# Attention and quantised feed-forward on one core: the exponentials' scores as one 72-row product a head, four heads' maxima in one run

## The chip, the cores and the metric

The kernel runs on one core of a Trainium2 chip. The time is device microseconds of one execution, and the number told is the median of several runs. TensorE multiplies into PSUM (8 banks of 128 partitions x 512 f32), ScalarE and VectorE read PSUM, GpSimd works on SBUF alone, and transfers are issued from the queues of SyncE (SP) and GpSimd (POOL).

## The reference

One pre-norm transformer layer on x of 2 x 1024 x 512 in f32, with 32 heads of 16 columns, and a feed-forward part of 1376 columns with ternary weights and rounded activations:

```python
x = x + attn(layernorm(x), w_q, w_k, w_v, w_o)
x = x + ffn(layernorm(x), w_gate, w_up, w_down, s_gate, s_up, s_down)

# attn
q, k, v = (proj(w_q), proj(w_k), proj(w_v))          # b, 32 heads, 1024, 16
scores = einsum('bhqd,bhkd->bhqk', q, k) / sqrt(16.)
attn = softmax(scores, axis=-1)
out = einsum('bhqk,bhkd->bhqd', attn, v)             # then w_o
# ffn
xq = int4_quant(x)
gate = square(relu(bitlinear(xq, w_gate, s_gate)))
inter = int8_quant(bitlinear(xq, w_up, s_up) * gate)
return bitlinear(inter, w_down, s_down)
```

## The kernel before

The attention is cut into 32 **steps**: two batches, two halves of 512 queries, four groups of 128 columns (8 heads), and in each group two sets of four heads (s = 0 and 1). A step is cut into 8 **slots** (`NT`). The main loop counts slots with T. In slot T it does three things for three places in the row of steps:

- **Maxima** of step T // 8. For each head the scores of 128 queries by 512 keys are made (`max_mm`, L590), and VectorE reduces two heads at once, 128 x 1024, to the negated row maxima (`max_reduce`, L600). After eight slots `max_parts` joins the pieces into `mcols`, and `max_rows` (L613, L617) turns them into rows with four products against the identity and a ScalarE copy `mrow`.
- **Exponentials** of the step that had slot T - 10 (`LE`). The scores are made again the other way round, 128 keys by 512 queries, the maximum is subtracted in the same accumulation, and ScalarE takes the exponential of two heads at once (`exp_mm` L630, `exponentials` L634). `j` = 0 is heads 0 and 1, `j` = 1 heads 2 and 3.
- **Values** (`weigh_values`, L660) for the exponentials of slot T - 1: for each of four heads the 128 keys by 32 columns of `vt` are multiplied with the exponentials, accumulated over the eight slots in one PSUM bank (`pso`); columns of ones beside the values give the denominators.

Numbers are split into a high and a low part (`hi`, `lo`) in the format f32r, which TensorE takes in one pass; plain f32 takes more. For each head `kst` holds 32 rows: 16 of the high part of k and 16 of the low part. `qst[n][0]` and `qst[n][1]` hold the high and the low part of q, each twice. So a score is two products of 32 rows, and four heads lie in four 32-row tiles of the array. The subtraction of the maximum is a third product of two rows, `onesr` by `mrow`. The parts come from DRAM (`kD`, `qD`), where the projections put them, by `load_k` (L567) and `load_q` (L573).

The order on every engine is the order in which the program emits instructions (a manual schedule). A slot before is:

1. `scores(exps[:1], maxs[:1])`: exponentials j = 0 mixed with maxima of heads 2 and 3 in three passes.
2. `weigh_values` of the slot before.
3. `scores(exps[1:], maxs[1:])`: exponentials j = 1 mixed with maxima of heads 0 and 1.
4. In the first slot of a new step `max_parts`, in the second `max_rows`.
5. **Fillers** (`fill.run`): pieces of all other work, the projections (L476, L533), layer norms, output projection (L847) and feed-forward (L937, L1006), handed out by a budget of 960 to 1800 ns a slot and by due times in slots. Their products go to a PSUM bank of their own, and ScalarE, VectorE or GpSimd take them from there.

Score tiles come from a ring of three, each of two banks (`scores_psum`). Loads for a step are emitted some five slots ahead (`load_slot`), on SP's queue, where the stores of projections, the small transfers of `normalise` and the transposes of the feed-forward part stand as well. At the end `the_end` finishes the last 512 tokens in an order of its own, in buffers that it takes over from the loop (`place`).

Of the kernel before, what the change touches and what calls it, by code (L numbers as in the profile page):

```python
# [10 lines left out]
F32 = mybir.dt.float32  # L11
# [5 lines left out]
ALU = mybir.AluOpType  # L17
# [216 lines left out]
def kernel(  # L234
# [65 lines left out]
    nc.vector.tensor_copy(onesr, eye)  # L300
    ones = onesr.bitcast(F32)

    lowrow = const.tile([P, 1], F32, name="lowrow")
    nc.vector.memset(lowrow, -1.0)
    for i in range(4):
        nc.vector.memset(lowrow[32 * i : 32 * i + 16, :], 0.0)
    second = const.tile([P, 1], I32, name="second")
    nc.vector.memset(second, 1)
    for i in range(4):
# [1 line left out]
    negmagic = const.tile([P, 1], F32, name="negmagic")  # L311
    nc.vector.memset(negmagic, -MAGIC)

    mcols = [const.tile([P, TQ, P], F32R, name=f"mcols{k}") for k in range(2)]
    vst = [const.tile([P, 2, 4, 4, 32], F32, name=f"vst{k}") for k in range(1)]
    for m in mcols:
        nc.gpsimd.memset(m.bitcast(F32), 0.0)
    for v in vst:
        for s in range(2):
            nc.gpsimd.memset(v[:, s, :, :, 16 * (1 - s) : 16 * (1 - s) + 16], 1.0)  # L320
# [15 lines left out]
    def scores_psum(name):  # L336
        return ps_s.tile([P, 2, QB], F32, tag="s", name=name)
# [29 lines left out]
    def norm_inputs(b, half, fast, need=()):  # L367
# [45 lines left out]


    qD = {
        (b, g, h): dram.tile([2, 8 * 32, QB], F32, name=f"qD_{b}_{g}_{h}")
        for b in range(B)
        for g in range(NG)
        for h in range(NQ)
    }  # L420
    kD = {(b, g): dram.tile([8 * 32, S], F32, name=f"kD_{b}_{g}") for b in range(B) for g in range(NG)}
    vD = {
        (b, g, s): dram.tile([P, NT, P], F32, name=f"vD_{b}_{g}_{s}")
        for b in range(B)
# [35 lines left out]
    def project_qk(b, g, which, h, have, fast=False, first=False):  # L460
# [34 lines left out]
        if first:  # L495

            for s in range(2 - which):
                for l, part in enumerate((hi, lo)):
                    for a in range(2 - which):
                        for r in range(4):  # L500
                            src = part[32 * r + 16 * s : 32 * r + 16 * s + 16, :].bitcast(F32)
                            at = 32 * r + 16 * (l if which else a)
                            dst = kst[0][:, h * QB : (h + 1) * QB] if which else qst[s][l]
                            queue = (nc.sync, nc.gpsimd)[l if which else a]
                            queue.dma_start(dst[at : at + 16, :].bitcast(F32), src)  # L505
                yield ("copied",)
            if which == 0:
                return
        queue = nc.gpsimd if fast and not first else nc.sync
        for l, part in enumerate((hi, lo)):  # L510
            if which == 0:
                dst = qD[b, g, h][l].rearrange("(e a d) q -> a e d q", a=2, d=16)
                for a in range(2):
                    queue.dma_start(dst[a], part.bitcast(F32))
            else:
                dst = kD[b, g].rearrange("(e l d) q -> l e d q", l=2, d=16)[l]
                queue.dma_start(dst[:, :, h * QB : (h + 1) * QB], part.bitcast(F32))
            yield ("gap", 1)

    def step_k(n):  # L520
        b, _, g, s = steps[n]
        return kD[b, g].rearrange("(r s e) q -> s r e q", r=4, s=2)[s]

    def project_v(b, g, half, have):
        w, wait = proj_weights("v", b, g, f"wv_{b}_{g}_{half}")
# [34 lines left out]
    pm, mrow, probs = {}, {}, {}  # L560

    def places(n):
        kst[n] = sb.tile([P, S], F32R, tag="kst", name=f"kst_{n}", bufs=3)
        qst[n] = [sb.tile([P, QB], F32R, tag="qst", name=f"qst_{n}_{l}", bufs=6) for l in range(2)]

    def load_k(n, first=0):
        nc.sync.dma_start(kst[n][:, first:].bitcast(F32), step_k(n)[:, :, first:])  # L567
# [1 line left out]
    def load_q(n):  # L569
        b, h, g, s = steps[n]  # L570
        for l, q in enumerate(qst[n]):
            rows = qD[b, g, h][l].rearrange("(r s e) q -> s r e q", r=4, s=2)[s]
            nc.sync.dma_start(q.bitcast(F32), rows)  # L573

    def load_v(n):
        b, h, g, s = steps[n]
# [25 lines left out]
    def max_parts(n):  # L602
        m = sp.tile([P, TQ, 4], F32, tag="m", name=f"m_{n}")
        p = pm.pop(n)
        nc.vector.tensor_tensor(m, p[:, :, 0, :], p[:, :, 1, :], ALU.min)
        cols = mcols[n % 2].rearrange("p t (r c) -> p t r c", r=4)
        nc.vector.tensor_copy(cols[:, :, :, 0], m)
        nc.vector.tensor_tensor(cols[:, :, :, 1], m, cols[:, :, :, 0].bitcast(F32), ALU.subtract)

    def max_rows(n):  # L610
        ps = scores_psum(f"psn_{n}")[:, 0, :]
        for t in range(TQ):
            nc.tensor.matmul(  # L613
                ps[:, t * P : (t + 1) * P], mcols[n % 2][:, t, :], identr, start=True, stop=True
            )
        mrow[n] = sb.tile([P, QB], F32R, tag="mrow", name=f"mrow_{n}", bufs=2)
        nc.scalar.copy(mrow[n], ps)  # L617

    probs = {}

    def exp_mm(n, i, j, ps, l):
        for r in (2 * j, 2 * j + 1):
            rows = slice(32 * r, 32 * r + 32)
            if l < 2:
                left, right = kst[n][rows, i * P : (i + 1) * P], qst[n][l][rows, :]
            else:

                rows = slice(32 * r, 32 * r + 2)
                left, right = onesr[rows, :], mrow[n][rows, :]
            nc.tensor.matmul(ps[:, r % 2, :], left, right, start=(l == 0), stop=(l == 2))  # L630

    def exponentials(n, i, j, ps):
        e = sb.tile([P, 2, QB], F32, tag="e", name=f"e_{n}_{i}_{j}", bufs=4)
        nc.scalar.activation(e, ps, AF.Exp, scale=SCALE)  # L634
        probs.setdefault((n, i), {})[j] = e

    def scores(exps, maxs):


        es = [(*x, scores_psum(f"pse_{x[0]}_{x[1]}_{x[2]}")) for x in exps]  # L640
        ms = [(*x, max_tile(*x)) for x in maxs]
        for l in range(3):
            for x in es:
                exp_mm(*x, l)
            if l or not es:
                for x in ms:
                    max_mm(*x, l - bool(es)) if l - bool(es) < 2 else None
        for x in es:
            exponentials(*x)
        for x in ms:  # L650
            max_reduce(*x)

    acc, po, OT = {}, {}, {}

# [95 lines left out]
    def load_raw(m, i, name):  # L750
        ap, parts = mats[m]
        c, n, rows, cols = parts[i]
        t = sb.tile([P, 512], F32, tag="raw", name=f"{name}{m}_{c}_{n}", bufs=4)
        nc.gpsimd.dma_start(t[:rows, :cols], ap[c * P : c * P + rows, n : n + cols])
        return t

    def weight_sums():
# [2 lines left out]
            nc.gpsimd.memset(wsum[m], 0.0)  # L760
        todo = [(m, i) for m in range(3) for i in range(len(mats[m][1]))]
        raw = deque()
        for k in range(len(todo) + 4):
            if k >= 4:
                m, i = todo[k - 4]
                c, n, rows, cols = mats[m][1][i]
                junk = sb.tile([P, 512], BF16, tag="junk", name=f"junk{m}_{i}", bufs=1)
                nc.scalar.activation(
                    junk[:rows, :cols],
                    raw.popleft()[:rows, :cols],  # L770
                    AF.Abs,
                    accum_out=wsum[m][:rows, i : i + 1],
                )
            if k < len(todo):
                raw.append(load_raw(*todo[k], "raw"))
            yield ("gap", 1)
# [266 lines left out]
    def the_end(n):  # L1043
# [74 lines left out]
        def place(tag, shape, k, bufs):  # L1118
            return [sb.tile(shape, F32, tag=tag, name=f"end_{tag}_{j}", bufs=bufs) for j in range(k)]

        quad = [t.bitcast(BF16) for t in place("qst", [P, QB], TQ, 6)]
        xqs, xT = [q[:, :H] for q in quad], [q[:, H:].rearrange("p (c t) -> p c t", c=KC) for q in quad]
        xns = place("raw", [P, 512], TQ, 4)
        v = place("inter", [P, I], 2, 2)
        for half in range(2):
            v.append(place(f"xnT{half}", [P, KC * QB], 1, 1)[0][:, :I])
        iq = [sb.tile([P, FC * P], BF16, tag="iq", name=f"end_iq_{j}", bufs=2) for j in range(2)]
        iq += [t.bitcast(BF16)[:, :I] for t in place("v", [P, NT * P], 2, 2)]
        pairs = place("e", [P, 2, QB], 4, 4)
        iqT = [t.bitcast(BF16)[:, : FC * P] for t in place("kst", [P, S], 3, 3)]  # L1130
        iqT.append(pairs.pop().rearrange("p j q -> p (j q)").bitcast(BF16)[:, : FC * P])
        g2 = [t[:, j, :] for t in pairs for j in range(2)]

        def inputs(i):
# [151 lines left out]
    ps = scores_psum("warm")  # L1286
    for k in range(WARM):
        nc.tensor.matmul(
            ps[:, k % 2, :], onesr, mcols[0].rearrange("p t c -> p (t c)"), start=True, stop=True
        )  # L1290
    fill.kind = "s"
    now(firsts[0])
# [107 lines left out]
    for T in range(LE + NT * NSTEP + 1):  # L1400
# [4 lines left out]

        fill.scores = int(T < LE - 1 or T >= NT * NSTEP)

        n = T // NT + 1
        if 1 < n < NSTEP and T == load_slot(n):
            b, h, g, s = steps[n]  # L1410
# [8 lines left out]
            load_v(n)  # L1419
        if im == 0 and 0 < nm <= NSTEP:  # L1420
            max_parts(nm - 1)
        exps = [(ne, ie, j) for j in range(2)] if 0 <= ne < NSTEP else []
        maxs = [(nm, im, j) for j in (1, 0)] if nm < NSTEP else []
        mixed = bool(exps and maxs)
        if mixed:
            scores(exps[:1], maxs[:1])
        elif exps:
            scores(exps, [])
        if 0 <= nw < NSTEP:
            weigh_values(nw, iw)  # L1430
            if iw == NT - 1 and nw % 2 and nw < NSTEP - 1:
# [3 lines left out]
                fill.add("tokens", first_tokens(nw), (), "ffn", 0)  # L1435
        feed()
        fill.run(100.0, short=True)
        if mixed:
            scores(exps[1:], maxs[1:])
        elif maxs:  # L1440
            scores([], maxs)
        if im == 1 and 0 < nm <= NSTEP:
            max_rows(nm - 1)
        share = min(max(fill.pace([w[4:] for w in ffns]), SHARE), MORE)
        left = fill.run(share + min(left, SHARE))

    while ffns or fill.left():
        feed()
# [49 lines left out]
```

## Time and profile before

| | before |
|---|---|
| median of 3 runs | 1179.4 us (1176.8 to 1182.54) |
| span of the profiled execution | 1179.7 us |
| TensorE busy | 1154.8 us, 98% |
| VectorE busy | 868.8 us, 74% |
| ScalarE busy | 686.8 us, 58% |
| GpSimd busy | 264.1 us, 22% |
| bytes moved by DMA | 135.35 MB |
| mean granted TensorE clock | 0.999 |

The profiled execution has no time of its own beside its span; the span lies within the three times. Busy time of TensorE is modelled at its ends, and products in different tiles of the array overlap, so the sum of its groups' durations is more than its busy time; starts of instructions are a better measure. In the rows of groups, the numbers behind the bar are busy time and mean duration in ns, and behind the second bar the idle time of the engine just before, with what ended it. `PEld` is TensorE's loading of weights.

### The profile page before, as it was taken

The page shows a single profiled execution, that of the slowest core. Times are in us where ns is not written, and L with a number is a line of the kernel's source. Part 1 is how long each engine was busy: PE and PEld are TensorE (multiplying, and loading weights), DVE is VectorE, ACT ScalarE, POOL GpSimd, SP SyncE. Part 2 cuts the span into 40 slices and gives each one's busy share as a digit, 9 for nine tenths or more (in the row PEclk, how much of TensorE's full clock was granted, in tenths as well). Part 3 has the DMA queues.
Part 4 walks back from the last instruction along what each step waited for, and adds up shares of the span by engine and source line. Part 5 has one row for each costly group of instructions (what it writes and reads, how often), then busy time and mean ns, then how long its engine had stood idle before and what let it go on. Part 6 is the DMA issues. An engine that isn't in the chain of part 4 may idle for free.

```text
span 1179.7 us, 21990 instructions
## 1 busy us (share of the span) xinstructions
PE 1154.8 (98%) x8922; PEld 522.5 (44%) x8922; DVE 868.8 (74%) x1261; ACT 686.8 (58%) x878; POOL 264.1 (22%) x319
## 2 busy tenths in 40 slices
PE   8899999999999999999999999999999999999998
PEld 5454444544444444544444445444444433444344
DVE  6765577898876677788866665786988788888467
ACT  2058765556565556566665555465666555665746
POOL 3224336465501101221011011022110001220111
PEclk9999999999999999999999999999999999999999
DMA  5666765556623323443633324244442516362300
GB/s 157 174 183 194 249 197 176 172 190 197 194 93 96 103 55 110 113 95 77 94 86 121 124 59 147 84 130 138 84 97 60 89 53 83 58 81 55 79 9 37
DMA packets 97099, 135.35 MB, mean 115 GB/s; under 512 B 34829, under 2 KB 54285, under 8 KB 96997
## 3 DMA queue, kind: packets, MB, share of 16 engines
q1 hardware_dynamic: 87204, 105.75, 34.6%
q0 software_dynamic: 9792, 28.19, 7.7%
q8 instruction: 70, 1.15, 0.4%
q14 instruction: 33, 0.26, 0.1%
HBM read 89.25 MB, written 37.19 MB: 107 GB/s over the span
## 4 chain that ended last, share of the span: by engine, by line
PE 81%; DVE 5%; DMA 5%; issue 2%; POOL 2%; SPq 2%; ACT 2%; POOLq 0%; DVEq 0%; ACTq 0%
PE pse L630 25%; PE pso L660 18%; PE psm L590 9%; PE psv L533 4%; PE psk L476 4%; PE psy L847 4%; PE psq L476 4%; PE pu L937 2%; PE py L1006 2%; DVE pm L600 2%; PE pg L937 2%; DMA rden<-rD 1%; PE psn L613 1%; SPq L505 1%; PE end L1161 1%
## 5 line engine op out<-in xcount | busy, mean ns | idle before, releaser
L600 DVE TENSOR_REDUCE pm<-psm 128x2 f32<-128x1024 f32 x512 | 623.8, 1222 | 242.9 <-PE pse L630 146.0
L634 ACT ACTIVATE e<-pse 128x1024 f32<-128x1024 f32 x512 | 522.7, 1023 | 408.2 <-PE pse L630 307.3
L590 PE MATMUL psm<-kst,qst 32*128 32x512 f32 x2048 | 369.5, 444 | 7.3 <-DMA kst<-kD 3.8
L630 PE MATMUL pse<-qst,kst 32*128 32x512 f32 x2048 | 367.6, 442 | 3.9 <-DVE pm L600 3.1
L630 PEld LDWEIGHTS pse<-qst,kst 32*128 32x128 f32 x2048 | 149.2, 183 | 332.8 <-issue 199.7
L660 PE MATMUL pso<-e,v 128*32 128x512 f32 x2048 | 272.9, 605 | 0.0
L630 PE MATMUL pse<-mrow,onesr 2*128 2x512 f32 x1024 | 203.9, 396 | 0.0
L590 PEld LDWEIGHTS psm<-kst,qst 32*128 32x128 f32 x2048 | 151.3, 183 | 25.5 <-ACT e L634 10.8
L630 PEld LDWEIGHTS pse<-mrow,onesr 2*128 2x128 f32 x1024 | 94.5, 183 | 3.3
L951 POOL TENSOR_TENSOR g<-g 128x460 f32<-128x460 f32 (+1 forms) x36 | 34.7, 964 | 244.7 <-ACT g L947 237.4
L660 PEld LDWEIGHTS pso<-e,v 128*32 128x32 f32 x2048 | 40.4, 108 | 94.4 <-issue 93.7
L807 POOL TENSOR_SCALAR low<-raws,whalf 128x512 bf16<-128x512 f32 (+2 forms) x35 | 52.0, 1488 | 30.5 <-DMA raws<-in_wuT 8.1
L476 PE MATMUL psq<-xnT,wq 128*128 128x512 f32 x112 | 57.8, 626 | 0.0
L533 PE MATMUL psv<-wv,xnT 128*128 128x128 f32 x384 | 53.2, 285 | 0.0
L533 PEld LDWEIGHTS psv<-wv,xnT 128*128 128x128 f32 x384 | 45.9, 191 | 12.5 <-issue 11.7
L847 PE MATMUL psy<-wo,OT 128*128 128x512 f32 x96 | 49.6, 625 | 0.0
L476 PE MATMUL psk<-xnT,wk 128*128 128x512 f32 x96 | 49.5, 624 | 0.0
L699 POOL TENSOR_TENSOR OT<-po,rden 128x512 f32<-128x512 f32 x15 | 19.2, 1278 | 99.5 <-PE pse L630 52.8
L547 POOL DMA_DIRECT2D vD<-vst x30 | 16.7, 559 | 110.5 <-ACT vst L545 107.8
L909 POOL TENSOR_SCALAR xn<-x,mv,a 128x512 f32<-128x512 f32 x12 | 25.1, 2089 | 71.5 <-DVE a L885 71.5
L937 PEld LDWEIGHTS <-xqT 128*128 128x128 bf16 x288 | 22.4, 98 | 37.8 <-issue 23.8
L937 PE MATMUL pg<-wg,xqT 128*128 128x460 fp8e4 (+1 forms) x144 | 34.2, 360 | 0.0
(227 smaller groups left out, 945.1 us busy)
## 6 DMA issues: line engine op xcount, KB each, us to landing
v<-vD SPq DMA_DIRECT2D x32, 512.0 KB
kst<-kD SPq DMA_DIRECT2D x31, 512.0 KB
qst<-qD SPq DMA_DIRECT2D x60, 256.0 KB
vD<-vst POOLq DMA_DIRECT2D x30, 256.0 KB, 5.7
qD<-hi_q SPq DMA_DIRECT2D x28, 256.0 KB
qD<-lo_q SPq DMA_DIRECT2D x28, 256.0 KB
x<-in_x SPq DMA_DIRECT2D x20, 256.0 KB
rden<-rD SPq DMA_DIRECT2D x15, 256.0 KB
```

What stands on the lines that cost most here:

```text
L476: nc.tensor.matmul(ps, w[:, c, :], xnT[b, h][:, c, :], start=(c == 0), stop=(c == KC - 1))
L533: nc.tensor.matmul(ps[:, i * P : (i + 1) * P], xnT[b, half][:, c, i * P : (i + 1) * P], w[:, c, :], start=(c == 0), stop=(c == KC - 1),)
L590: nc.tensor.matmul(ps[:, r % 2, :], qst[n][l][rows, t * P : (t + 1) * P], kst[n][rows, kh * QB : (kh + 1) * QB], start=(l == 0), stop=(l = ...
L600: nc.vector.tensor_reduce(pm[n][:, t, kh, 2 * j : 2 * j + 2], ps, AX.X, ALU.max, negate=True)
L630: nc.tensor.matmul(ps[:, r % 2, :], left, right, start=(l == 0), stop=(l == 2))
L634: nc.scalar.activation(e, ps, AF.Exp, scale=SCALE)
L660: nc.tensor.matmul(acc[n][32 * r : 32 * r + 32, :], vt[n][:, i, r, :], e[r // 2][:, r % 2, :], start=(i == 0), stop=(i == NT - 1),)
L807: nc.gpsimd.tensor_scalar(low, w, h[:rows, m, 1:2], None, ALU.is_lt)
L847: nc.tensor.matmul(ps, OT[b, h, g][:, i * P : (i + 1) * P], wo[g], start=(g == 0), stop=(g == NG - 1),)
L909: nc.gpsimd.tensor_scalar(xn, xt, mean, a, ALU.subtract, ALU.mult)
L937: nc.tensor.matmul(ps, xT[:, c, :], w[:, c, n : n + size], start=(c == 0), stop=(c == KC - 1))
L951: nc.gpsimd.tensor_tensor(g2[j], g2[j], g2[j], ALU.mult)
```

## The change

The exponentials' scores of a head become one product of 72 rows. For this k is stored twice in `kD` (`a` = 0, 1) and q with its parts in one tile, so that 64 rows hold high and low of k, twice, against high of q twice and low of q twice: all four parts of the score in one contraction. Eight more rows subtract the maxima: rows 64 to 71 of `qm` hold the maxima rows of all four heads (copied by ScalarE, four times side by side), and the same rows of `kw` hold ones for the head's own pair and zeros for the others (`subtraction_rows`, once). `kw` holds two slots' keys for four heads and is loaded every second slot, two slots ahead; `qm` is loaded once a step.

The maxima stay products of 32 rows, but all four heads are made in one run. The order in a slot is now maxima, values of the slot before, exponentials j = 0, `max_rows` (in a step's first slot), fillers, exponentials j = 1. `kst` has 2 buffers where it had 3, `qst` 4 where it had 6, `e` 2 where it had 4, `raw` 3 where it had 4, `mcols` 1 where it had 2; the first query's parts are stored to `qD` as well; and `the_end` takes other buffers.

```diff
-    mcols = [const.tile([P, TQ, P], F32R, name=f"mcols{k}") for k in range(2)]
+    MROW = 64
+    mcols = const.tile([P, TQ, P], F32R, name="mcols")
...
             else:
-                dst = kD[b, g].rearrange("(e l d) q -> l e d q", l=2, d=16)[l]
-                queue.dma_start(dst[:, :, h * QB : (h + 1) * QB], part.bitcast(F32))
+                dst = kD[b, g].rearrange("(e a l d) q -> l a e d q", a=2, l=2, d=16)[l]
+                for a in range(2):
+                    queue.dma_start(dst[a][:, :, h * QB : (h + 1) * QB], part.bitcast(F32))
...
+    kw = [const.tile([P, 4, 2 * P], F32R, name=f"kw{k}") for k in range(2)]
...
+    def subtraction_rows():
+
+        pick = sp.tile([P, 4], F32, tag="rstd1", name="pick")
+        pairs = ident[:, MROW : MROW + 8].rearrange("p (r c) -> p r c", c=2)
+        nc.vector.tensor_reduce(pick, pairs, AX.X, ALU.add)
+        src = pick[MROW : MROW + 8, :].rearrange("p (r o) -> p r o", o=1)
+        for k in kw:
+            nc.vector.tensor_copy(k[MROW : MROW + 8, :, :], src.to_broadcast([8, 4, 2 * P]))
+
+    def load_kw(n, p):
+
+        b, h, g, s = steps[n]
+        src = kD[b, g].rearrange("(r s e) q -> s e r q", r=4, s=2)[s][:, :, 2 * P * p : 2 * P * (p + 1)]
+        nc.sync.dma_start(kw[p % 2][:64].bitcast(F32), src)
+
+    def load_qm(n):
+
+        b, h, g, s = steps[n]
+        qm[n] = sb.tile([P, 4, QB], F32R, tag="qm", name=f"qm_{n}", bufs=2)
+        src = qD[b, g, h].rearrange("(r s e) q -> s e r q", r=4, s=2)[s]
+        nc.sync.dma_start(qm[n][:64].bitcast(F32), src)
...
-        mrow[n] = sb.tile([P, QB], F32R, tag="mrow", name=f"mrow_{n}", bufs=2)
-        nc.scalar.copy(mrow[n], ps)
+        rows = ps[MROW : MROW + 8, :].rearrange("p (o q) -> p o q", o=1)
+        nc.scalar.copy(qm[n][MROW : MROW + 8, :, :], rows.to_broadcast([8, 4, QB]))
...
-    def exp_mm(n, i, j, ps, l):
+    def exp_mm(n, i, j, ps):
+        k = kw[(i // 2) % 2]
         for r in (2 * j, 2 * j + 1):
...
-            nc.tensor.matmul(ps[:, r % 2, :], left, right, start=(l == 0), stop=(l == 2))
+            nc.tensor.matmul(
+                ps[:, r % 2, :],
+                k[: MROW + 8, r, (i % 2) * P : (i % 2 + 1) * P],
+                qm[n][: MROW + 8, r, :],
+                start=True,
+                stop=True,
+            )
...
+    def maxima(n, i):
+
+        ms = [(n, i, j, max_tile(n, i, j)) for j in range(2)]
+        for l in range(2):
+            for x in ms:
+                max_mm(*x, l)
         for x in ms:
             max_reduce(*x)
+
+    def weights_of(n, i, j):
+
+        ps = scores_psum(f"pse_{n}_{i}_{j}")
+        exp_mm(n, i, j, ps)
+        exponentials(n, i, j, ps)
...
+        if im == 4 and nm < NSTEP:
+            load_qm(nm)
+        n, p = divmod(T + 2 - LE, NT)
+        if 0 <= n < NSTEP and p % 2 == 0:
+            load_kw(n, p // 2)
...
-        if mixed:
-            scores(exps[:1], maxs[:1])
-        elif exps:
-            scores(exps, [])
+        exps = 0 <= ne < NSTEP
+        if nm < NSTEP:
+            maxima(nm, im)
         if 0 <= nw < NSTEP:
             weigh_values(nw, iw)
...
         fill.run(100.0, short=True)
-        if mixed:
-            scores(exps[1:], maxs[1:])
-        elif maxs:
-            scores([], maxs)
-        if im == 1 and 0 < nm <= NSTEP:
+        if exps:
+            weights_of(ne, ie, 0)
+        if im == 0 and 0 < nm <= NSTEP:
             max_rows(nm - 1)
         share = min(max(fill.pace([w[4:] for w in ffns]), SHARE), MORE)
         left = fill.run(share + min(left, SHARE))
+        if exps:
+            weights_of(ne, ie, 1)
```

## The prediction

> **What bounds the kernel now.** I read the page's busy times first, then its idle times by group, then the timeline of one slot, and last the timelines of two places at the start where operations that the change multiplies already stand alone.
>
> ```profile
> span 1179.7 us, 21990 instructions
> PE 1154.8 (98%) x8922; PEld 522.5 (44%) x8922; DVE 868.8 (74%) x1261; ACT 686.8 (58%) x878; POOL 264.1 (22%) x319
> ...
> L600 DVE TENSOR_REDUCE pm<-psm 128x2 f32<-128x1024 f32 x512 | 623.8, 1222 | 242.9 <-PE pse L630 146.0
> L634 ACT ACTIVATE e<-pse 128x1024 f32<-128x1024 f32 x512 | 522.7, 1023 | 408.2 <-PE pse L630 307.3
> L590 PE MATMUL psm<-kst,qst 32*128 32x512 f32 x2048 | 369.5, 444 | 7.3 <-DMA kst<-kD 3.8
> L630 PE MATMUL pse<-qst,kst 32*128 32x512 f32 x2048 | 367.6, 442 | 3.9 <-DVE pm L600 3.1
> ```
>
> TensorE is busy 98% of the span and its score groups sat idle 7.3 and 3.9 us in all: nothing is waited for. VectorE and ScalarE wait for TensorE. So a change pays by TensorE time taken from a slot, and costs by every wait that it puts into TensorE's order. One slot, TensorE and ScalarE:
>
> ```profile
> 606.81 0.51 PE L630 MATMUL pse<-qst,kst 32*128 32x512 f32 x2
> 606.82 0.50 PE L590 MATMUL psm<-kst,qst 32*128 32x512 f32 x2
> 607.14 0.40 PE L630 MATMUL pse<-qst,kst 32*128 32x512 f32 x2
> 607.16 0.40 PE L590 MATMUL psm<-kst,qst 32*128 32x512 f32 x2
> 607.38 0.40 PE L630 MATMUL pse<-mrow,onesr 2*128 2x512 f32 x2
> 607.70 1.06 PE L660 MATMUL pso<-e,v 128*32 128x512 f32 x8
> ...
> 607.87 1.02 ACT L634 ACTIVATE e<-pse 128x1024 f32<-128x1024 f32 x1 [2.64 <-PE pse L630]
> 608.70 0.50 PE L630 MATMUL pse<-qst,kst 32*128 32x512 f32 x2
> ```
>
> Starts count here, not durations (first column; the ends are modelled and overlap). A half slot of scores is three passes of 512 columns: the first takes 0.33 us (606.81 to 607.14), the second 0.24, the last 0.32 until the values' product starts. A pass in a run is about 0.23, so entering a new tile shape costs about 0.10 (its weights are loaded in the open) and leaving it about 0.10. Half slot 0.89, value product 1.00, second half 0.90 (608.70 to 609.60, where psk begins): 2.79 us. By the windows view the stretch 62 to 1093 us holds 246 slots, 4.19 us each, so 1.40 are left for fillers, with their own entry and exit (0.20) and max_rows.
>
> From the start of the kernel, three rows in three answers of the timeline:
>
> ```profile
> 32.03 0.74 PE L590 MATMUL psm<-kst,qst 32*128 32x512 f32 x8
> 32.69 2.05 PE L533 MATMUL psv<-wv_first,xnT 128*128 128x128 f32 x16
> ```
> ```profile
> 10.32 1.79 PE L1288 MATMUL warm<-mcols,onesr 128*128 128x512 f32 x7
> ```
> ```profile
> 63.98 1.02 ACT L634 ACTIVATE e<-pse 128x1024 f32<-128x1024 f32 x1 [0.32 <-PE pse L630]
> ...
> 65.06 0.51 PE L590 MATMUL psm<-kst,qst 32*128 32x512 f32 x2 [0.88 <-ACT e L634]
> ```
>
> The first is the changed maxima run itself: no exponentials run yet, and four heads take 0.66 us (32.03 to 32.69). The second is a whole-array product of 512 columns in the same number format: seven in 1.79, the last lasting 0.39, so (1.79-0.39)/6 = 0.23 apart, the same pass as a 32-row one. The third is a hand-over: the exponentials end at 65.00 or 65.01 and TensorE starts at 65.06, 0.05 later. In the slot above, ScalarE starts 0.49 after the start of the last product (607.38 to 607.87).
>
> **Products.** A slot now has maxima 0.66, values 1.00, exponentials j=0 entering a whole-array shape 0.33+0.23 = 0.56, fillers, j=1 with no entry 0.46 and 0.10 to leave: 2.78, as before. But the fillers are whole-array products too and lose their entry and exit: -0.20, so -0.21 a slot, 246 x 0.21 = -52 us. Weight loads of the second product of a pair I take as hidden, because psk's loads of 0.19 us lie under its 512-column passes; uncovered they would cost up to 0.10 on each of four products, +98 us (a rival below).
>
> A rule speaks against even this gain. The Trainium skill, "TensorE: Matmul & The Clock Gate", section "Measured speedup vs the span model", has four packed 32-row products of 512 columns running 3.07 times as fast as unpacked ones. By an estimate from that page, 20 small products before are 20/3.07 = 6.5 pass times and 8/3.07+4 = 6.6 after: no gain, and the whole sum would be some 50 us higher. The eight maxima in 0.66 us do not settle it, since they hold one entry and one exit.
>
> **The wait that the change adds.** weights_of(.., 1) is now the last thing of a slot, and weigh_values, which needs its exponentials for heads 2 and 3, follows in the next slot after the maxima run alone. Before, the fillers (1.40) and a half slot (0.89) lay between. Let j=1's first product start at 0. The second starts at 0.23, ScalarE at 0.23+0.49 = 0.72, ends 1.74, TensorE sees it at 1.80. TensorE leaves at 0.56, runs maxima 0.66 and reaches the values at 1.21. Heads 0 and 1 may start, heads 2 and 3 not before 1.80; they need two rounds of 0.43 after that (values' 1.00 less 0.10 to leave and 0.04 of entry) and 0.10 to leave: 1.80+0.85+0.10 = 2.75, where 2.21 was due. Cost 0.54 a slot, 246 x 0.54 = +132 us. Behind it on TensorE stand both exponentials' products and all fillers; nothing else is in its order to fill the hole. In the ten slots after the last maxima nothing covers it: some +1.2 each, +12.
>
> **Other ScalarE work ahead of j=1.** Its queue has 620.5 us in the 1031 us window, exponentials 246 x 2 x 1.023 = 503, so 0.48 a slot of others, pieces of 0.55 to 0.87. One that drains the last filler can start only after that product and ends at 0.8 to 1.1 on the clock above, against 0.72. I take +0.10 a slot, +25 (0 to 0.3, so 0 to 74).
>
> **max_rows.** Its ScalarE copy grows from 512 to 4 x 512 columns on 8 rows. From 0.58 us for 512 (L617) and 1.02 for 1024, 0.86 ns a column, I take 0.58+1536 x 0.00086 = 1.90; bounds 0.58, where the copied length should not count, and 2.05, two exponentials. Once in eight slots it stands between exponentials j=0 and j=1. From j=0's first product: exponentials 0.82 to 1.84, copy to 3.74; j=1's products end so that ScalarE was due at 0.56+0.44+1.04+0.72 = 2.76. About 1.0 later, 32 x 1.0 = +32 us (0 to 37). The second maxima tile of the next slot waits for the same copy, at the same time, so it isn't added. max_rows comes a slot earlier after max_parts, but behind maxima, values and j=0, 2.2 us against some 0.6 us of VectorE work: nothing.
>
> **VectorE and PSUM.** Both reductions (2 x 1.22) now come together. The ring of three score tiles gives j=1 the tile of the first maxima, free about 2.1 us after the run starts, and needed 2.8 or more after: nothing. Reductions and others are 775.2 of 1031 us: no bound.
>
> **Loads and stores.** Per step four kw loads of 256 KB and one qm of 512 KB, 48 MB in all, kD stores doubled, 8 MB, first query's stores 1 MB. The middle's DMA is 0.44 busy at 118 GB/s; with 57 MB more it is some 0.55. All go through SP's queue, behind kst and qst (1 MB, one slot ahead of qm): 1.8 MB at 118/0.44 = 268 GB/s is 6.7 us, while a kw load has two slots and 2.2 us, over 10 us. It waits for the last product of the slot before, and holds up what is behind it on SP (k, q, v loads with five slots of lead, normalise's and the output's transfers). Cost nothing; if that cover fails, see the rivals. At the start the first maxima of step 1 already wait 3.80 us for kst, and 1.5 MB more of stores go ahead of that load: at 158 (the first 62 us, 0.57 busy) to 277 GB/s 5 to 10 us, part of it beside other work; I take +6 (0 to 13). The smaller buffers (kst, qst, e, raw, mcols) are free by program order when taken again: e's by the values' product that stands ahead of the next exponentials. Set-up of kw's constant rows, removed memsets, the changed end buffers: nothing.
>
> **Sum** against the profiled execution's span of 1179.7 us (the three times have their median at 1179.4, so nothing lies around it): 1179.7 - 52 + 132 + 12 + 25 + 32 + 6 = 1334.7, 1335.
>
> **Rivals.** (1) *The wait stays hidden*, and fewer shape changes win: 1335-132-12-25 = 1166. It decides if the exponentials come back within 0.98 us of the start of their last product, when TensorE reaches the values (1.21-0.23); the rows have 0.49+1.02+0.05 = 1.56, so only a longer maxima run or other unseen work between could do it. Chance 0.05. (2) *kw comes late*: the first third of the span runs DMA at 0.5 to 0.7 already, and 43 of the 128 loads late by 2 us are +86: 1421. For it SP's long waits, against it the 10 us of lead. 0.10. (3) *Whole-array products wait for their weights*: +98, 1433; against it psk. 0.05. My forecast has 0.80; its own ends are 1179.7-52+132+5 = 1265 with all the small terms nothing (the last slots at 5), and 1179.7-52+132+15+74+37+13 = 1399.
>
> A difference of 0.5% is about what can be told from no change here. The range 1265 to 1400 leaves out rivals (1), (2) and (3) at 0.20. Faster 0.04, within 0.5% 0.01 (both from (1)), slower 0.95.
>
> **What would show it.** Right: in the timeline two or three of four slots with heads 2 and 3 of pso starting about 0.6 us after heads 0 and 1, released by ACT e; TensorE's busy share well under 98%; the ScalarE copy near 1.9 us; maxima run 0.66, an exponentials' pair 0.46 behind a filler. Wrong: no gap in pso, or gaps before pse named DMA kw, or whole-array pairs 0.33 apart.

## The result, and the profile after

The changed kernel takes 1546.7 us (median of four runs, 1544.9 to 1552.9) against 1178.1 before (median of four runs as well): a ratio of 1.313, with a 95% interval of 1.308 to 1.318. The forecast was 1335, with 1400 as its upper end. So the sign was right and the size was not: +155 us were forecast, and +371 appeared between the spans of the two profiled executions. The profiled execution of the changed kernel took 1552.9 us, with a span of 1551.2.

The page after, busy times and the costliest groups (busy time and mean ns of one behind the first bar, idle time just before them and its releaser behind the second):

```profile
span 1551.2 us, 18308 instructions
PE 1340.1 (86%) x6874; PEld 572.7 (37%) x6874; DVE 841.9 (54%) x1259; ACT 723.8 (47%) x878; POOL 266.3 (17%) x322
...
L620 DVE TENSOR_REDUCE pm<-psm 128x2 f32<-128x1024 f32 x512 | 602.9, 1219 | 545.5 <-PE psm L610 545.1
L654 ACT ACTIVATE e<-pse 128x1024 f32<-128x1024 f32 x512 | 524.3, 1026 | 684.1 <-PE pse L644 680.0
L644 PE MATMUL pse<-qm,kw 72*128 72x512 f32 x1024 | 433.4, 507 | 139.7 <-DMA kw<-kD 139.7
L679 PE MATMUL pso<-e,v 128*32 128x512 f32 x2048 | 440.2, 626 | 19.3 <-ACT e L654 19.1
...
L610 PE MATMUL psm<-kst,qst 32*128 32x512 f32 x2048 | 220.3, 469 | 40.7 <-ACT qm L637 14.7
L679 PEld LDWEIGHTS pso<-e,v 128*32 128x32 f32 x2048 | 73.6, 110 | 241.4 <-ACT e L654 144.3
...
L637 ACT CAST qm<-psn 8x2048 fp32r<-8x2048 f32 x32 | 59.4, 1858 | 6.8 <-PE psn L633 6.0
```

TensorE was hardly kept waiting before; now it is busy 86%. The largest named wait, 139.7 us before the exponentials' products (L644), is ended by the DMA of `kw`, the transfer that the forecast priced at nothing. The wait of the values' products for ScalarE, which was to be the main cost, shows 19.3 us only in their row (L679 PE). The timeline explains why that row is so small:

```profile
605.14 0.74 PE L610 MATMUL psm<-kst,qst 32*128 32x512 f32 x8
605.31 1.03 ACT L654 ACTIVATE e<-pse 128x1024 f32<-128x1024 f32 x1 [0.30 <-PE pse L644]
...
605.81 1.63 PE L679 MATMUL pso<-e,v 128*32 128x512 f32 x8
...
606.39 0.14 PEld L679 LDWEIGHTS pso<-e,v 128*32 128x32 f32 x4 [0.44 <-ACT e L654]
...
607.37 0.74 PE L644 MATMUL pse<-qm,kw 72*128 72x512 f32 x2
```

The values' products begin at 605.81, 0.67 after the start of the maxima run, and the next products begin at 607.37, 1.56 later; before it was 1.00. The exponentials of heads 2 and 3 end at 606.34 (605.31 + 1.03), and the products of those heads start with their weights, at 606.39. The wait lies inside the group of eight products, whose modelled busy time covers it, so the row of the products shows no idle time for it. A slot's length shows it, and so does the row of their weight loads (PEld): there ScalarE's exponentials end 144.3 us of idle time, where before they were not among the releasers of that row:

```profile
L660 PEld LDWEIGHTS pso<-e,v 128*32 128x32 f32 x2048 | 40.4, 108 | 94.4 <-issue 93.7
```

**Where the 371 us lie.** The table has the mean time from one slot's values to the next slot's, by the slot's place in its step (T modulo 8), 30 or 31 slots each, between T = 11 and T = 256. The last row is the median of an ordinary slot (T = 3 modulo 8).

| place | before | after | a_split | b_order | c_both | e_nowait | f_copy | g_apart | h_best |
|---|---|---|---|---|---|---|---|---|---|
| 0 | 4.36 | 6.14 | 6.10 | 5.78 | 5.41 | 5.68 | 5.14 | 6.31 | 5.46 |
| 1 | 4.48 | 4.52 | 4.46 | 4.08 | 3.86 | 3.88 | 4.53 | 4.50 | 3.91 |
| 4 | 4.17 | 4.91 | 4.74 | 4.25 | 4.18 | 4.12 | 4.68 | 5.96 | 4.22 |
| 6 | 4.08 | 10.53 | 5.23 | 12.04 | 5.29 | 5.89 | 5.31 | 4.64 | 4.30 |
| ordinary | 3.87 | 4.25 | 4.27 | 3.81 | 3.82 | 3.66 | 4.30 | 4.25 | 3.82 |

Place 6 alone costs 31 x (10.53 - 4.08) = 200 us of the 371. These 245 slots together grew from 1025.4 to 1358.6 us (+333); the time up to the first values' product grew by 16.2, the ten slots behind by 21, the end by 1.

**What happens at place 6.** `kw` for two slots is issued two slots ahead. The one that is used at place 6 is issued at place 4, right behind `kst`, the two `qst` and `qm`, on the same queue. SyncE's side of the timeline:

```profile
602.31 0.56 SPq L562 DMA_DIRECT2D kst<-kD  x1
602.91 1.10 SPq L568 DMA_DIRECT2D qst<-qD  x2
604.05 2.69 SPq L593 DMA_DIRECT2D qm<-qD  x1
...
610.32 0.60 SPq L586 DMA_DIRECT2D kw<-kD  x1
```

Here TensorE waits for that `kw` until 623.56, 13.2 us after its issue. Over all steps the median from issue to the products is 14.6 us at place 6, while the three other `kw` loads of a step are used a median of 11.5 to 14 us after issue, all but one without a wait. At place 6 TensorE waited in 24 of the 32 steps, 5.8 us on average. The windows of the same stretch (last columns: granted clock, DMA share, GB/s):

```profile
602.00:604.00 2.00, 2.00 (x11) 0.82 (x8) 2.00 (x2) 0.72 (x3) 0.00 (x0) 1.00 0.67 147
604.00:608.00 4.00, 4.00 (x23) 1.50 (x22) 2.14 (x3) 2.04 (x2) 0.00 (x0) 1.00 0.27 89
608.00:610.00 2.00, 2.00 (x7) 0.90 (x5) 1.06 (x3) 1.02 (x1) 0.00 (x0) 1.00 1.03 217
610.00:618.00 8.00, 8.00 (x45) 3.10 (x43) 5.41 (x5) 3.58 (x4) 0.00 (x0) 1.00 0.74 170
618.00:624.00 6.00, 3.40 (x21) 1.21 (x20) 3.72 (x8) 1.55 (x2) 0.00 (x0) 1.00 0.65 167
624.00:626.00 2.00, 2.00 (x5) 0.91 (x4) 0.00 (x0) 1.02 (x1) 0.62 (x1) 0.52 0.41 124
```

Two things are to be seen. While `kst` and `qst` are under way (604 to 608) the DMA engines work at a share of 0.27 and 89 GB/s: about a quarter of them. And after the wait the granted clock falls to 0.52, so that products take longer when data is there at last. The clock is below full for 226 us of the span (4.9 before); such a time begins within, or up to 3 us after, 28 of TensorE's 30 idle stretches of over 2 us. The same stretch in the timeline, with the wait in brackets:

```profile
623.56 0.76 PE L644 MATMUL pse<-qm,kw 72*128 72x512 f32 x2 [2.60 <-DMA kw<-kD]
...
625.03 1.84 PE L644 MATMUL pse<-qm,kw 72*128 72x512 f32 x2
...
626.80 1.03 PE L610 MATMUL psm<-kst,qst 32*128 32x512 f32 x8
```

A maxima run of 0.74 takes 1.03 there.

The packets of `kw` show the quarter directly. A load is 256 packets of 1 KB, a size that no other transfer of the trace has. For eleven of the loads used at place 6 they can be told from those of the next load. In seven of the eleven, 192 packets moved together and the other 64, a quarter, began 5.0 to 6.6 us later; in an eighth it was 1.2 us, and the other three had no such gap. The load issued at 699.57, for example, moved 192 packets from 700.95 to 702.96 and 64 from 707.95 to 710.92. The trace doesn't name a packet's engine, but the split is that of twelve engines that were free and four that were not.

The low share was there to be read before the change, around the same loads of the old kernel, in its windows:

```profile
594.00:598.00 4.00, 4.00 (x40) 1.76 (x38) 2.63 (x3) 3.64 (x6) 0.95 (x1) 1.00 0.26 95
598.00:601.00 3.00, 3.00 (x30) 0.99 (x22) 2.74 (x4) 2.00 (x3) 0.00 (x0) 1.00 0.72 216
601.00:605.00 4.00, 4.00 (x32) 1.76 (x32) 2.65 (x3) 2.69 (x4) 0.95 (x1) 1.00 0.26 101
```

At 95 to 101 GB/s the 1 MB of `kst` and `qst` takes some 10.5 us, where the forecast's 268 GB/s gives 3.9. In the changed kernel it is slower still: seven loads of `kst` whose packets stand apart in the trace took 7.2 to 8.9 us for their 512 KB.

### The profile page after: what moved, and what is told of

The parts are those of the page before. It is cut to its first block, busy times and chain, and to the rows that moved or that the text cites. A ratio compares the mean times of both kernels' runs of the same rounds, so it can differ in the third digit from the quotient of the medians.

```text
span 1551.2 us, 18308 instructions
## 1 busy us (share of the span) xinstructions
PE 1340.1 (86%) x6874; PEld 572.7 (37%) x6874; DVE 841.9 (54%) x1259; ACT 723.8 (47%) x878; POOL 266.3 (17%) x322
## 4 chain that ended last, share of the span: by engine, by line
PE 55%; DMA 25%; issue 9%; ACT 5%; SPq 3%; DVE 1%; POOL 1%; ACTq 0%; POOLq 0%; DVEq 0%
DMA kw<-kD 21%; PE pso L679 17%; PE pse L644 14%; PE psm L610 8%; PE psq L472 3%; PE psv L528 2%; ACT e L654 2%; PE psk L472 2%; PE py L1025 2%; ACT qm L637 2%; PE psy L866 2%; PE pu L956 1%; PE pg L956 1%; SPq L501 1%; DMA rden<-rD 1%
## 5 line engine op out<-in xcount | busy, mean ns | idle before, releaser
L620 DVE TENSOR_REDUCE pm<-psm 128x2 f32<-128x1024 f32 x512 | 602.9, 1219 | 545.5 <-PE psm L610 545.1
L644 PE MATMUL pse<-qm,kw 72*128 72x512 f32 x1024 | 433.4, 507 | 139.7 <-DMA kw<-kD 139.7
L679 PE MATMUL pso<-e,v 128*32 128x512 f32 x2048 | 440.2, 626 | 19.3 <-ACT e L654 19.1
L644 PEld LDWEIGHTS pse<-qm,kw 72*128 72x128 f32 x1024 | 180.2, 201 | 431.5 <-issue 407.7
L610 PE MATMUL psm<-kst,qst 32*128 32x512 f32 x2048 | 220.3, 469 | 40.7 <-ACT qm L637 14.7
L679 PEld LDWEIGHTS pso<-e,v 128*32 128x32 f32 x2048 | 73.6, 110 | 241.4 <-ACT e L654 144.3
L610 PEld LDWEIGHTS psm<-kst,qst 32*128 32x128 f32 x2048 | 91.2, 193 | 154.8 <-issue 98.2
L637 ACT CAST qm<-psn 8x2048 fp32r<-8x2048 f32 x32 | 59.4, 1858 | 6.8 <-PE psn L633 6.0
L979 DVE TENSOR_TENSOR inter<-pu,g 128x460 f32<-128x460 f32 (+1 forms) x36 | 22.8, 634 | 49.0 <-PE pu L956 48.8
L928 POOL TENSOR_SCALAR xn<-x,mv,a 128x512 f32<-128x512 f32 x12 | 25.4, 2117 | 89.8 <-DVE a L904 89.8
L956 PE MATMUL pu<-wu,xqT 128*128 128x460 fp8e4 (+1 forms) x144 | 36.6, 379 | 0.0
```

The costliest lines, as they stand in the source:

```text
L610: nc.tensor.matmul(ps[:, r % 2, :], qst[n][l][rows, t * P : (t + 1) * P], kst[n][rows, kh * QB : (kh + 1) * QB], start=(l == 0), stop=(l = ...
L620: nc.vector.tensor_reduce(pm[n][:, t, kh, 2 * j : 2 * j + 2], ps, AX.X, ALU.max, negate=True)
L637: nc.scalar.copy(qm[n][MROW : MROW + 8, :, :], rows.to_broadcast([8, 4, QB]))
L644: nc.tensor.matmul(ps[:, r % 2, :], k[: MROW + 8, r, (i % 2) * P : (i % 2 + 1) * P], qm[n][: MROW + 8, r, :], start=True, stop=True,)
L679: nc.tensor.matmul(acc[n][32 * r : 32 * r + 32, :], vt[n][:, i, r, :], e[r // 2][:, r % 2, :], start=(i == 0), stop=(i == NT - 1),)
L956: nc.tensor.matmul(ps, xT[:, c, :], w[:, c, n : n + size], start=(c == 0), stop=(c == KC - 1))
```

## The experiments

The theory behind them: `kw` is late because `kst` and `qst` use a quarter of the DMA engines and stand ahead of it in one queue; the rest is the forecast's wait of the values. The rival: `kw` costs by itself (the 48 MB, or SyncE's queue as such), or the order of the slot costs more than the forecast had. Times are medians, ratios are to the kernel before, run beside it on the same chip.

### a_split: the same loads in four pieces

```diff
-        nc.sync.dma_start(kst[n][:, first:].bitcast(F32), step_k(n)[:, :, first:])
+        for r in range(4):
+            nc.sync.dma_start(kst[n][32 * r : 32 * r + 32, first:].bitcast(F32), step_k(n)[r][:, first:])
```

and the same for `qst`. Nothing else differs: the same bytes, queue and place.

> The changed kernel with each load of kst and qst issued as four, one of 32 rows for each head; same bytes, same places in the order. Theory (queue): in the changed kernel the transfers of kst and qst run at about 100 GB/s with a DMA share of 0.26, a quarter of the engines, and the kw load for the slots at T = 6 of each eight stands behind that 1 MB in the same queue. Spread over all engines they are gone in under half the time, so that slot falls from 10.5 us to about 5 and the total to some 1360 us (1330 to 1400), with the granted clock back over 0.98. Rival (bytes): 60 MB more in all and short packets are what makes kw late; then nothing changes, 1500 us or more. Rival (lead): two slots are too few whatever stands ahead; 1450 or more.

Measured: 1360.0 us, ratio 1.153 (1.148 to 1.157), 187 us less than the changed kernel. The group of the exponentials' products, and the windows from the issue of `kst` at 543.20:

```profile
L646 PE MATMUL pse<-qm,kw 72*128 72x512 f32 x1024 | 412.1, 485 | 15.8 <-DMA kw<-kD 15.8
```

```profile
542.50:544.00 1.50, 1.50 (x11) 1.01 (x8) 1.11 (x1) 0.98 (x2) 0.00 (x0) 1.00 1.13 265
544.00:546.00 2.00, 2.00 (x17) 1.10 (x18) 0.16 (x1) 2.00 (x4) 0.00 (x0) 1.00 0.77 246
546.00:548.00 2.00, 2.00 (x15) 0.96 (x14) 2.00 (x2) 0.14 (x1) 0.00 (x0) 1.00 0.81 214
```

The wait falls from 139.7 to 15.8 us and place 6 from 10.53 to 5.23. The DMA share in these windows is 0.77 to 1.13. Their 214 to 265 GB/s count other transfers too, which now run beside `kst`: its own packets still moved from 544 to 550, and issuing the twelve pieces took SyncE 8.5 us (543.20 to 551.72) instead of 1.7. What the split takes away is the late quarter: in the five loads of `kw` at place 6 whose packets can be told apart here, no gap between packets is over 0.24 us. The unsplit load walks in DRAM over 4 heads first, then over rows. The Trainium skill, "DMA: Bandwidth & Descriptors", section "Why a DMA increments its semaphore by 16 and not by 1", says that the number of DMA engines is the largest up to 16 that divides the slowest dimension of both sides. The trace agrees: 4 of 16 is what the 0.26 to 0.27 of the unsplit loads show, and by the same rule a piece of 32 rows takes all 16.

Between the spans of the two profiled executions lie 192 us, 164 of them at place 6. Idle time for `kw` explains 124 of these. The other 40 I put down to the halved clock (time below full clock: 226 us to 33), which is a subtraction and was not measured by itself.

### d_nokw: the loads of kw left out

```diff
-        nc.sync.dma_start(kw[p % 2][:64].bitcast(F32), src)
+        if n == 0 and p < 2:
+            nc.sync.dma_start(kw[p % 2][:64].bitcast(F32), src)
```

> The changed kernel without 126 of its 128 loads of kw: the exponentials' scores are made with the first keys throughout, the rest is as it is. Theory (queue): what the loads cost is what the one late load in four costs; about 1350 us (1320 to 1390), within 2% of the kernel with split loads. Rival (bytes): 32 MB less frees other waits as well, more than 5% under the split kernel.

Measured: 1369.1 us, ratio 1.159 (1.156 to 1.163). The 245 slots take 1177.8 us here and 1178.5 in a_split: with the split, 32 MB of loads cost these slots next to nothing in all. So it is not the bytes that cost, but the landing of one load in four. The two agree in the sum alone: `kst` and `qst` are not split here, and place 6 is 20 us shorter than in a_split, places 0 and 5 together 19 us longer.

### g_apart: kst and qst moved, not split

`kst` is loaded two slots earlier (`T == NT * n - 7`) and `qst` two later (`T == NT * n - 3`).

> The changed kernel with its loads unsplit, but kst's issued two slots earlier and qst's two slots later, so that 0.5 MB instead of 1 MB stands ahead of a kw load. Bytes and engines are the same. Theory (queue): no kw load finds more than 5 us of four-engine transfer ahead of it, 1360 to 1400. Rival (four engines' bandwidth, wherever the loads stand): 1450 or more.

Measured: 1417.5 us, ratio 1.202 (1.197 to 1.206), between the two. Place 6 is cured (4.64), and place 4 rises from 4.91 to 5.96, because the load of `kw` for it stands behind `kst` now: four loads there came late, by 2.9 to 14.2 us, the two longest in the first 300 us. The lateness follows the slow loads to where they are put: this speaks for the queue, and against a fault of place 6.

### i_kwpool: kw on GpSimd's queue

```diff
-        nc.sync.dma_start(kw[p % 2][:64].bitcast(F32), src)
+        nc.gpsimd.dma_start(kw[p % 2][:64].bitcast(F32), src)
```

> The changed kernel with the kw loads issued on GpSimd's queue instead of SP's, nothing else moved; kst and qst stay unsplit on four engines. Theory (order in the queue): a kw load is late because it stands behind 1 MB in SP's own queue; on another queue it passes that by, the slot at T = 6 falls to about 5 us and the total to 1350 to 1420. Rival (the four engines themselves): kw's packets on those four engines still share them with kst and qst, and GpSimd's own waits come on top; 1480 or more.

Measured: 1427.5 us, ratio 1.208 (1.203 to 1.214), just above the theory's range. TensorE's idle time for `kw` falls to 21.8 us and place 6 to 5.52, with `kst` and `qst` as slow as ever: a median of 8.2 us from issue to landing for that load on a queue without them, and of 10.7 until TensorE uses it, where it was 14.6. What is gained is partly lost elsewhere, since the issue now waits on GpSimd's queue for TensorE to let go of the buffer, and GpSimd's own work stands behind it. Its waits (us in all, times, longest):

```profile
POOL kw L586 <- PE pse L644: 415.9, 68, 15.6
```

### e_nowait: the wait of the values taken away

On a_split: the values' products of heads 2 and 3 read the exponentials of heads 0 and 1, which have long been there.

```diff
-                e[r // 2][:, r % 2, :],
+                e[0][:, r % 2, :],
```

> The kernel with split loads (1360 us), and the values of all four heads taken from the exponentials j=0; those of j=1 are still made, but nothing reads them (heads 2 and 3 come out wrong). It prices the wait for j=1 with the order kept. Theory: 0.54 us in each of 246 slots, 1.2 in the last ten, 0.1 of other ScalarE work and part of the 1.0 at the copy of the maxima rows go: 160 to 200 us less, 1160 to 1200; shorter slots may give up to 30 of it back to the kw loads. Rival (the wait only takes the place of another one, a PSUM tile or a reduction): 1300 or more.

Measured: 1258.9 us, ratio 1.070 (1.064 to 1.076). An ordinary slot falls from 4.27 to 3.66: this is the price of the wait, and it leaves a slot shorter than the 3.87 before by 0.21. Yet the whole gained 101 us, not the 160 or more that were expected. In shorter slots the lead of two slots is shorter, and `kw` comes late again (45.4 us of idle time in all):

```profile
701.11 0.74 PE L612 MATMUL psm<-kst,qst 32*128 32x512 f32 x8
...
701.78 1.07 PE L681 MATMUL pso<-e,v 128*32 128x512 f32 x8
...
705.78 1.19 PE L646 MATMUL pse<-qm,kw 72*128 72x512 f32 x2 [2.94 <-DMA kw<-kD]
```

The values take 1.07 instead of 1.63 (701.78), and the next exponentials with a new `kw` wait 2.94 us. Place 6 rises from 5.23 to 5.89 where it should have fallen by 0.6: 31 x 1.26 = 39 us. A wait that hides a transfer is not worth its length when it is removed.

### b_order: exponentials j = 1 ahead of the fillers

```diff
+        if exps:
+            weights_of(ne, ie, 1)
         share = min(max(fill.pace([w[4:] for w in ffns]), SHARE), MORE)
         left = fill.run(share + min(left, SHARE))
-        if exps:
-            weights_of(ne, ie, 1)
```

on the changed kernel, without the split.

> The changed kernel with the exponentials j=1 made ahead of the fillers instead of after them. Theory: the wait of the values for them (about 0.55 us a slot, and some 1.0 more at the copy of the maxima rows) is then covered by fillers and maxima; the base slots fall from about 4.25 to 3.7 and the total by 100 to 170 us, to 1380 to 1450; the wait for kw stays or grows, as shorter slots leave it less lead. Rival: the wait for kw swallows all of it, 1520 or more.

Measured: 1505.0 us, ratio 1.274 (1.269 to 1.279), between the theory's range and the rival's. Ordinary slots fall from 4.25 to 3.81 and place 6 rises to 12.04:

```profile
L644 PE MATMUL pse<-qm,kw 72*128 72x512 f32 x1024 | 342.9, 453 | 208.3 <-DMA kw<-kD 191.6 <-DVE pm L620 16.4
```

0.44 a slot over 245 slots is 108 us, and 42 came out. Idle time for `kw` rose by 52 us, and the time below full clock from 226 to 290 us.

### c_both: the split, and both exponentials together

On a_split: `weights_of(ne, ie, 1)` directly behind j = 0, `max_rows` and the fillers after them.

> Both edits: loads of kst and qst by head, exponentials j=1 straight after j=0, and max_rows behind both. Theory: neither wait is left; 1180 less 52 for fewer changes of tile shape, plus 16 at the start, so 1130 to 1200 us. Rival (bytes): the wait for kw stays, 1350 or more.

Measured: 1283.6 us, ratio 1.089 (1.084 to 1.093), well over the 1130 to 1200 expected. Ordinary slots reach 3.82, not 3.66:

```profile
645.95 1.28 PE L681 MATMUL pso<-e,v 128*32 128x512 f32 x8
...
647.16 1.21 PE L646 MATMUL pse<-qm,kw 72*128 72x512 f32 x4
...
648.00 1.94 ACT L656 ACTIVATE e<-pse 128x1024 f32<-128x1024 f32 x2 [1.87 <-PE pse L646]
```

ScalarE needs 1.94 us for the two exponentials in a row, with the wait for their products in front; the values start to start (645.95 to 647.16) take 1.21, above the 1.00 before. And the exponentials' products wait for reductions and keys:

```profile
L646 PE MATMUL pse<-qm,kw 72*128 72x512 f32 x1024 | 318.9, 430 | 52.3 <-DMA kw<-kD 25.8 <-DVE pm L622 25.4 <-ACT qm L639 0.5
```

The second pair of products comes so early that the score tile which it takes over has not been reduced yet (`pm`, 25.4 us). The forecast had put this wait at nothing, rightly for the order of the change; with both pairs together it appears.

### f_copy: the copy of the maxima rows cut short

On a_split: ScalarE copies 512 columns, and GpSimd spreads them three times.

```diff
-        nc.scalar.copy(qm[n][MROW : MROW + 8, :, :], rows.to_broadcast([8, 4, QB]))
+        m = qm[n][MROW : MROW + 8, :, :]
+        nc.scalar.copy(m[:, 0:1, :], rows)
+        nc.gpsimd.tensor_copy(m[:, 1:4, :], m[:, 0:1, :].bitcast(F32).to_broadcast([8, 3, QB]))
```

> The kernel with split loads, the copy of the maxima rows cut to 512 columns on ScalarE, and GpSimd spreading them to the other three heads' places. Theory: the ScalarE copy falls from 1.86 to 0.58 us and the slot at T = 0 of each eight from 6.0 to about 4.8, 31 x 1.2 = 37 us less: 1310 to 1335. Rival (GpSimd's spread comes too late for the first exponentials two slots on, or the copy isn't in the way): 1350 or more.

Measured: 1345.4 us, ratio 1.140 (1.136 to 1.144), more than the 1310 to 1335 expected. The tile's own rows (duration in ns, least, median and most):

```profile
L640 ACT CAST qm<-psn x32: 577/577/580, 65.6 to 1240.5; 8x512 fp32r<-8x512 f32 x32
L641 POOL CAST qm<-qm x32: 1456/1457/1747, 66.3 to 1241.2; 8x1536 fp32r<-8x1536 f32 x32
```

ScalarE's copy falls from 1.86 to 0.58 us, and place 0 from 6.10 to 5.14, 0.96 a step or 29 us in all. The total gained half of it: 6 us are lost before the first values' product, and some in other slots. Why was not settled.

### h_best: all of it together

On c_both: f_copy's copy, the joining of the maxima at the end of a step, and the loads of `kw`, `qm`, `kst` and `qst` moved apart.

> All together: split loads, kst's and qst's two slots later and qm's two slots earlier, kw's ahead of the others in a slot; exponentials j=1 straight after j=0; max_parts at the end of a step, the short copy of maxima rows with GpSimd's spread. Theory: no wait is left but about 0.2 us a slot for two exponentials in a row; 1180 - 52 + 50 + 16 at the two ends = 1194 at most, 1140 at least. Rival (loads of 48 MB more are late wherever they stand): 1250 or more.

Measured: 1255.5 us, ratio 1.064 (1.061 to 1.067), the best of the new form, and still 6% slower than before; the rival's figure, not the theory's. Place 6 is nearly cured (4.30), but the 245 slots keep 50 us over the kernel before, 33 of them at place 0 and 17 at place 2, the start 14.6 and the ten last slots 8.7. The windows view of 70 to 270 us shows what may be behind part of it, a DMA share of 0.84 (0.63 before in the same stretch) and a clock of 0.93:

```profile
70.00:270.00 200.00, 183.72 (x1091) 91.92 (x1084) 115.73 (x134) 112.16 (x180) 85.00 (x114) 0.93 0.84 232
```

That is argued, not shown: no run took the bytes away in this form.

### j_before_split: only the split, in the kernel before

> The kernel before with its loads of kst and qst split by head, as in the first experiment. Theory: those loads have five slots of lead there and nothing waits behind them but one load at the start (3.80 us for the second step's kst), so 0 to 5 us less: within 0.5%. Rival: the slow loads cost the kernel before as well; 10 us or more less. If it is faster, it is the version to keep.

Measured: 1175.6 us (12 runs), ratio 0.9952 (0.9930 to 0.9974). The first values' product comes at 62.5 us instead of 67.7, as the wait of 3.8 us for the first `kst` is gone; the slots are as before, for nothing in them waited for a load. The gain is half a per cent, with an interval that stays under 1. This is the fastest version measured here.

## Why the prediction was wrong in size and right in its other steps

**The step that failed: "Cost nothing" for the loads.** The working divided 1.8 MB by 268 GB/s, the mean rate over the mean share. The transfers that stood ahead of `kw` do not run at that rate: they used a quarter of the engines, and both the profile before and the runs show it. At 7.2 to 8.9 us for 512 KB, 1 MB is some 14 to 18 us (an estimate from the packets of `kst`), against the 6.7 us that the working had for all 1.8 MB. In the place shown, `kst` was issued at 602.31, the last quarter of `kw` did not move before 619.97, and TensorE had it at 623.56. The lead of "over 10 us" was there, a median of 11.5 to 14 us at the other places, and didn't cover this. The rival that names this (*kw comes late*) was there with a chance of 0.10, at 43 loads late by 2 us. It is 24 of the 32 loads at place 6, late by 5.8 us on average, and the clock, by the subtraction above, adds a third of that again. Price of this step: 187 us, the difference of a_split to the change.

**What a_split leaves** is what the rest of the sum described: 1335 forecast, 1360 measured. By its terms:

- *The wait of the values*, 0.54 a slot and 0.10 for ScalarE's other work: about right. e_nowait gives 4.27 - 3.66 = 0.61 for both.
- *The products*, -0.21 a slot: right. e_nowait's slot is 3.66 against 3.87 before. The estimate from the Trainium skill, "TensorE: Matmul & The Clock Gate", section "Measured speedup vs the span model", which spoke against it with no gain in the products, isn't borne out by this slot.
- *`max_rows`*: the copy took 1.86 us (1.90 forecast), and f_copy prices its added length at 0.96 a step (1.0 forecast).
- The 245 slots of a_split took +153; the terms for them give -52+132+25+32 = +137. Places 2 to 5 and 7 are 0.43 longer on average, as the terms say (-0.21+0.54+0.10). Place 6 holds 22 us more than that, since `kw` still comes late in six steps, each time after an issue that was 4 to 12 us late itself, and places 0 and 1 hold 6 less than their terms.
- *The start*, +6, and *the last ten slots*, +12: a_split has +7.8 and +18.0, the unsplit change +16.2 and +21.0. Both were too small.

**The rivals.** That the wait stays hidden is refuted: heads 2 and 3 start 0.58 us after heads 0 and 1 in the slot shown (606.39 less 605.81), and about 0.6 was forecast. Uncovered weight loads were not seen: they would have added 0.40 to a slot (98 us in 246), and e_nowait's ordinary slot is as long as the sum without them gives (3.87 - 0.21). That VectorE's reductions cost nothing held for the order of the change.

**The forecast's own signs.** Of what the text named as proof of error, "gaps before pse named DMA kw" came true, 139.7 us of them. Signs of being right came true beside it: heads 2 and 3 started 0.58 us after heads 0 and 1, the copy took 1.86 us, a maxima run 0.67. TensorE's busy share fell as well, to 86%, but mostly for another reason than the forecast's: it is 95% in a_split, where the wait of the values is the same.

## What to carry to other kernels

Before a load with a short lead is added, list what stands ahead of it in its own queue, and read the DMA share and the GB/s in the windows of those very transfers: a share near 0.25 meant a quarter of the engines here, and the mean rate hid it. When a step is moved to the end of a slot, look at who uses its result first in the next one; when a wait inside a slot is taken out, every transfer timed in slots loses as much lead. And look for the cost of a wait that lies inside a group of products in the length of the slot and in the row of the weight loads, not in the idle time before the products.

## What the hardware showed that was not expected

- Transfers whose outermost dimension in DRAM is 4 heads moved 89 to 101 GB/s at a DMA share of 0.26 or 0.27, and the `kw` load behind them in the queue mostly had a quarter of its packets 5.0 to 6.6 us after the rest. With one transfer a head the share was 0.77 to 1.13, and no such gap was over 0.24 us.
- A wait of over 2 us mostly cost twice: with 28 of 30 such waits in the changed kernel the granted clock of TensorE went to half, for stretches of 3.4 to 17.1 us. In all it lay under full for 226 us in the changed kernel and for 290 in b_order, against 4.9 before.
- Issuing a transfer behind the unsplit loads could take long: the issue of `qm` took 0.62 to 0.87 us in 18 steps and 1.9 to 6.2 in the other 14 (2.69 at 604.05 above), and SyncE issued nothing else in that time. In a_split it took 1.3 us at most.
